# Layer 0: weighing in parts, the image's group norm as its own task, TensorE's chunk work in text order

## The chip, the cores and the metric

The kernel runs on one core of a Trainium2 chip. The metric is the device time of one execution in microseconds, from the runs shown below. All data is 32-bit floating point. The core's engines are TensorE (PE, with its weight load PEld), VectorE (DVE), ScalarE (ACT), GpSimd (POOL) and SyncE (SP), which here issues all data transfers. Each engine works through its own instruction list strictly in order and waits on semaphores for the others.

## The reference

The model has four layers on 16 images of 192 channels and 32 by 32 pixels, each `x = x + layer(group_norm(x))`. The change touches layer 0 alone. Cut to what matters, layer 0 computes for each image (1024 tokens, 12 heads of 32):

```python
x = group_norm(x)                          # 32 groups of 6 channels
h = layernorm(seq)                         # over the 192 channels of a token
x_in, z = split(h @ w_up + b_up)           # 384 each
x_act = silu(causal_conv4(x_in))
q, k, v = x_act @ w_q, x_act @ w_k, x_in
i_pre, f_pre = [q, k, v] @ w_i + b_i, [q, k, v] @ w_f + b_f
# per head and token t:
m   = max(log_sigmoid(f) + m_old, i)
C   = exp(log_sigmoid(f) + m_old - m) * C_old + exp(i - m) * v k^T
n   = the same with k alone
hs  = (C q) / max(|n q|, 1)
hs  = normalise each head of hs;  h_out = (hs + skip * x_act) * silu(z)
x1  = seq + h_out @ w_down + b_down;       x2 = silu(seq @ w_lin + b_lin)
y   = conv3x3(x1 + x2);  batch norm over all images;  leaky relu
```

The other three layers are a selective scan, a depthwise convolution with batch norm, and a four-way selective scan with a local branch.

## The kernel before

**Tiling.** The recurrence of layer 0 is computed in chunks of 128 tokens: 8 an image, 128 in all. Within a chunk the recurrence is a masked, weighted product like attention; between chunks a state of 32 by 33 per head is carried (the 33rd column carries the denominator). Four chunks make a *unit* of 512 tokens (`U`), two units an image. What comes ahead of the recurrence is computed by unit (`layer0_front`): layer norm, `w_up`, the causal convolution `xact` on VectorE (12 passes), `w_lin`, the SiLUs (with two loads of the activation table), `w_q`, `w_k` and the gates (`layer0_gates`). The first unit of an image first loads the image into the tile `x`, of which there is one buffer, and normalises it by groups in place: statistics on VectorE, two small TensorE products (`gnmv`, `gnq`), a power on GpSimd, two passes over `x`.

**One step.** `layer0_step(g)` is one chunk. In the text it has, in order:
- the products `p = s * e` on VectorE, four of them, and `vr = v * e[..., 127]` on GpSimd;
- `layer0_weigh` for chunk g+1: a transfer of the gate row, spread over 128 partitions, into `e` (two buffers); two GpSimd additions (the mask, then `u` of each source token); an Exp on ScalarE;
- with a new unit also `layer0_decays`, eight tiny transposes and three tiny products on TensorE;
- `it = q * state` of the chunk before, then twelve products `num = p * v`, then `h` on VectorE;
- `layer0_state`: `vr * kt` on TensorE, four VectorE instructions for the new `state`;
- `layer0_scores` for chunk g+1: twelve products `s` (k times q), the transposes `kt` and `xin` with their evictions to `kt` (VectorE) and `v` (ScalarE);
- `layer0_output` for chunk g-1: the transposes of `hs`, the products with the gate, `ht`;
- `layer0_norm`: the head norm of `h`: sums on VectorE, `hs` (subtraction) on GpSimd, `sq` on ScalarE, `mhv` on VectorE and ScalarE, `hs` (multiplication) on GpSimd.

When a unit's last chunk is two steps old, `layer0_down` multiplies by `w_down` and writes the image into `ypad`. After an image's two units `layer0_spread` copies `ypad` through memory into `ya` and `yb`, and `layer0_conv2` does the 3 by 3 convolution as 15 taps in three parts.

**What sets the order.** The code does not issue instructions directly: it records them in text order, and a scheduler at compile time writes each engine's list. It goes by text order and by an estimate of when each operand is ready, so that an instruction may be moved ahead of others of its engine. The recorded text order itself comes from two sources. The steps of the chunks are the main line; between their parts (at each `yield`), `Side.tick` advances background tasks. A task is a generator with a kind, a start and an end, counted in steps; it gets its share of parts by the time passed, and `Wait` holds it back. Unit i's front runs from step 4i - 3.9 to 4i - 1.2, an image's convolution over 7.2 steps:

```python
side.add("front", self.layer0_front(i, sp, bp, dp, psum), NCH * i - 3.9, NCH * i - 1.2)
```

**PSUM.** Eight banks: two of `mm`, through which nearly all TensorE results go, four of `s`, one of `num`, one of `conv`. A group that writes `mm` needs the bank of the `mm` group two before it to be read out. `p` has three buffers for four products of a chunk, so that the fourth waits for the first three `num` products.

Of the kernel before, what the change touches and what calls it, by code (L numbers as in the profile page):

```python
# [10 lines left out]
F32 = mybir.dt.float32  # L11
AF = mybir.ActivationFunctionType
# [7 lines left out]
HP = 96  # L20
DI = 384
S = 1024
# [219 lines left out]


class Chunk:

# [15 lines left out]
class Program:  # L261
# [117 lines left out]
    def layer0(self):  # L379
        tc = self.tc  # L380
        with (
# [23 lines left out]
            self.layer0_weigh(chunks[0], bp)  # L405
            finish(self.layer0_scores(chunks[0], bp, psum))
# [80 lines left out]
    def layer0_conv2(self, b, part, bp, psum):  # L487
# [169 lines left out]
    def layer0_decays(self, unit, sp, psum):  # L657

        nc = self.nc
        ps = psum.tile([128, 512], F32, name="mm")  # L660
        u, w = unit["u"].rearrange("p (c t) -> p c t", c=NCH), unit["w"]
        for c in range(NCH):
            for j, t in enumerate((u, w)):
                o = (2 * c + j) * NH
                nc.tensor.transpose(ps[:, o : o + NH], t[:, c], self.k("ident", NH)[:, :NH])
        n = 2 * NCH * NH
        for t in range(3):
            nc.tensor.matmul(
                ps[:, n + t * NCH : n + (t + 1) * NCH], self.k0("sel", NH)[:, t * 128 : (t + 1) * 128], w[:, :, 127],
                start=True, stop=True,  # L670
            )
        uw = unit["uw"] = sp.tile([128, NCH, 2, NH], F32, name="uw")
        nc.vector.tensor_copy(uw, ps[:, :n].rearrange("p (c j h) -> p c j h", c=NCH, j=2))
        dec = unit["dec"] = sp.tile([128, 3, NCH], F32, name="dec")
        nc.vector.tensor_copy(dec, ps[:, n : n + 3 * NCH].rearrange("p (g c) -> p g c", g=3))

    def layer0_weigh(self, k, bp):

        nc = self.nc
        e = k.e = bp.tile([128, NH, 128], F32, name="e")  # L680
        nc.sync.dma_start(e, k.unit["row"][:, k.tok].partition_broadcast(128))
        nc.gpsimd.tensor_tensor(e, e, self.k0("mask")[:, None, :].to_broadcast([128, NH, 128]), ADD)  # L682
        nc.gpsimd.tensor_tensor(e, e, k.unit["uw"][:, k.c, 0][:, :, None].to_broadcast([128, NH, 128]), ADD)  # L683
        nc.scalar.activation(e, e, AF.Exp)  # L684

    def layer0_scores(self, k, bp, psum):
# [5 lines left out]
        for i in range(3):  # L692
            for j in range(4):
                part = slice(32 * j, 32 * j + 32)
                nc.tensor.matmul(k.s[j][:, i], k_[part, i, k.tok], q[part, i, k.tok], start=True, stop=True)
        yield
        k.kt = bp.tile([128, DI], F32, name="kt")
        ps = psum.tile([128, 512], F32, name="mm")
        for t in range(3):
            nc.tensor.transpose(ps[:, t * 128 : (t + 1) * 128], k_[:, t, k.tok], self.k("ident"))  # L700
        nc.vector.tensor_copy(k.kt, ps[:, :DI])
# [3 lines left out]
        for t in range(3):  # L705
            nc.tensor.transpose(
                ps[:, t * 128 : (t + 1) * 128], xin[:, t, 3 + k.tok.start : 3 + k.tok.stop], self.k("ident")
            )
        nc.scalar.copy(k.v[:, :, :DH], ps[:, :DI].rearrange("p (h d) -> p h d", h=NH))
        yield  # L710

    def layer0_step(self, g, n, chunks, sp, bp, psum):
# [8 lines left out]
        if k:  # L721
# [7 lines left out]
            if g + 1 < n:  # L729
                i, c = divmod(g + 1, NCH)  # L730
                new = chunks[g + 1] = Chunk(self.unit[i], c, g + 1)
                if c == 0:
                    self.layer0_decays(new.unit, sp, psum)
                self.layer0_weigh(new, bp)
            yield
            it = None
            if g % (S // 128):
                it = psum.tile([128, 512], F32, name="mm")
                for i in range(3):
                    nc.tensor.matmul(  # L740
                        it[:, i * 132 : (i + 1) * 132], k.unit["q"][:, i, k.tok], chunks[g - 1].state[:, i],
                        start=True, stop=True,
                    )
                h = bp.tile([128, NH, DH + 1], F32, name="h")
# [5 lines left out]
            for j in range(4):  # L750
                for i in range(3):
                    nc.tensor.matmul(num[:, 4 * i + j], p[j][:, i], k.v[:, 4 * i + j], start=True, stop=True)  # L752
# [17 lines left out]
    def layer0_state(self, k, vr, last, bp, psum):  # L770
# [3 lines left out]
        for i in range(3):  # L774
            nc.tensor.matmul(
                ps[:, i * 132 : (i + 1) * 132], k.kt[:, i * 128 : (i + 1) * 128],
                vr[:, 4 * i : 4 * i + 4].rearrange("p j d -> p (j d)"), start=True, stop=True,
            )
        new = k.state = bp.tile([128, 3, 132], F32, name="state")
# [32 lines left out]
    def layer0_output(self, k, bp, psum):  # L812
# [6 lines left out]
        for t in range(3):  # L819
            nc.tensor.transpose(  # L820
                ps[:, t * 128 : (t + 1) * 128], k.hs[:, 4 * t : 4 * t + 4].rearrange("p h d -> p (h d)"), self.k("ident")
            )
        nc.vector.tensor_tensor(
# [4 lines left out]
    def layer0_down(self, unit, psum):  # L828
# [5 lines left out]
        for m in range(2):  # L834
            ps = psum.tile([128, 512], F32, name="mm")
            for k in range(3):
                nc.tensor.matmul(
                    ps[:HP], self.w_down[:, k, m * HP : (m + 1) * HP], unit["ht"][:, k], start=k == 0, stop=k == 2
                )
            nc.vector.scalar_tensor_tensor(  # L840
# [839 lines left out]
```

## Time and profile before

| | |
|---|---|
| median of 3 runs | 17599.51 us (17563.52 to 17607.73) |
| the profiled execution: time | 17603.62 us |
| the profiled execution: span, first to last instruction | 17601.8 us |
| mean granted TensorE clock over the span | 0.943 |
| first and last start of a `num` product | 111.0 and 3981.7 us |
| first instruction of layer 1's scan (L955) | 4159.6 us |

The profile is of one execution. A page gives the busy time of each engine, its share in 40 slices, the costliest groups of instructions and who ended the idle time before them. Windows give the same for any stretch, with the clock that TensorE was granted. The waits name the waiting instruction, the one that released it, the total, how often, and the longest. The timeline gives instructions in order: start, duration, engine, line, tiles out<-in, count, and in brackets the idle time before and its releaser. `L726` is line 726 of the kernel. A TensorE product on 32-bit data shows as two passes, so twelve `num` products are 24 matmuls. Layer 0 fills about the first 4000 us; layers 1 to 3 follow in the rest.

### The profile page before, as it was taken

What the parts mean: (1) busy time and instruction counts of PE and PEld (TensorE: products, weight loads), DVE (VectorE), ACT (ScalarE), POOL (GpSimd) and SP (SyncE); (2) the same over time, 40 slices, a digit from 0 to 9 for tenths busy, and PEclk for the clock granted to TensorE, in tenths of its full rate; (3) what the DMA queues carried; (4) which work ended last, traced back from release to release, by engine and by line L of the source; (5) the groups of instructions that cost most, each with busy time, mean ns of one, the idle gap of its engine ahead of it and who ended that gap; (6) DMA issues with size and microseconds to landing.
All of it is one profiled execution on the core that took longest, in us unless ns stands there. A gap on an engine that the chain in (4) does not pass through costs nothing. (4 is left out here: it accounts for less than half of the span.)

```text
span 17601.8 us, 263080 instructions
## 1 busy us (share of the span) xinstructions
PE 15936.2 (91%) x99452; PEld 11143.2 (63%) x99452; DVE 13342.1 (76%) x14859; ACT 11884.1 (68%) x19637; POOL 11481.6 (65%) x5555
## 2 busy tenths in 40 slices
PE   8988898897988899878999999999999999999998
PEld 4444444444555555546777777777777777777777
DVE  4445554555777777757888888888988888888888
ACT  2222222224666666647888888888888888888888
POOL 3333333333555555546888888788888888888888
PEclk7888888888999999989999999999999999999999
DMA  1111111113333333333233233323323332333232
GB/s 48 40 41 40 44 41 36 41 44 92 119 118 118 115 114 112 109 105 101 94 105 105 86 99 107 98 91 99 107 90 97 101 108 83 99 107 100 90 98 67
DMA packets 890141, 1544.65 MB, mean 88 GB/s; under 512 B 83472, under 2 KB 314653, under 8 KB 879530
## 3 DMA queue, kind: packets, MB, share of 16 engines
q1 hardware_dynamic: 888874, 1527.81, 28.7%
q8 instruction: 788, 12.91, 0.3%
q14 instruction: 479, 3.92, 0.1%
HBM read 1284.22 MB, written 243.27 MB: 87 GB/s over the span
## 5 line engine op out<-in xcount | busy, mean ns | idle before, releaser
L986 POOL TENSOR_TENSOR h<-h,cb 128x1536 f32<-128x1536 f32 x2560 | 8875.8, 3471 | 1423.7 <-DVE h L979 894.0
L955 ACT ACTIVATE da<-dt,neg_a 128x512 f32<-128x512 f32 x7680 | 5266.4, 714 | 1725.5 <-DVE h L979 1658.1
L979 DVE TENSOR_TENSOR_SCAN h<-da,carry,xb 128x512 f32<-128x512 f32 x3840 | 4651.8, 1262 | 648.6 <-PE xb L966 589.4
L997 PE MATMUL y<-const,h 128*128 128x128 f32 x30720 | 4714.3, 276 | 129.4 <-DVE ysum L1437 54.4
L979 DVE TENSOR_TENSOR_SCAN h<-da,xb 128x512 f32<-128x512 f32 x3840 | 4440.2, 1202 | 387.9 <-PE xb L966 270.4
L963 PE MATMUL xb<-const,xbt 128*128 128x128 f32 x23040 | 4072.7, 282 | 417.6 <-DVE h L979 262.7
L935 ACT ACTIVATE xbt<-ut,bt 128x384 f32<-128x384 f32 x7680 | 4174.0, 603 | 242.1 <-PE xb L963 240.4
L963 PEld LDWEIGHTS xb<-const,xbt 128*128 128x128 f32 x23040 | 2755.9, 143 | 1812.2 <-issue 641.9
L997 PEld LDWEIGHTS y<-const,h 128*128 128x128 f32 x30720 | 3682.1, 143 | 322.5 <-issue 264.9
L966 PE MATMUL xb<-diag,ut 128*128 128x128 f32 x15360 | 3015.1, 278 | 0.0
L966 PEld LDWEIGHTS xb<-diag,ut 128*128 128x128 f32 x15360 | 2382.4, 195 | 63.2 <-issue 63.2
L985 POOL COPY carry<-h 128x3 f32<-128x3 f32 x1280 | 251.0, 196 | 1213.9 <-DVE h L979 952.7
L945 POOL TENSOR_TENSOR diag<-const,bt 128x512 f32<-128x512 f32 x640 | 681.8, 1065 | 544.1 <-PE xb L966 348.1
L799 POOL TENSOR_TENSOR hs<-h,mhm 128x384 f32<-128x384 f32 x128 | 108.2, 845 | 1068.3 <-DVE den L804 558.6
L682 POOL TENSOR_TENSOR e<-e,const 128x1536 f32<-128x1536 f32 x128 | 452.4, 3534 | 333.5 <-DMA e<-row 309.2
L684 ACT ACTIVATE e<-e 128x1536 f32<-128x1536 f32 x128 | 189.5, 1481 | 631.4 <-POOL e L683 631.4
L500 PE MATMUL conv<-ya,w_conv 128*64 128x512 f32 (+1 forms) x1152 | 578.6, 706 | 27.8 <-ACT y L506 21.3
L885 PE MATMUL mm<-dbl,w_dt 45*128 45x512 f32 x960 | 534.7, 641 | 33.6 <-DVE v L1459 16.2
L752 PEld LDWEIGHTS num<-v,p 128*128 128x128 f32 x3072 | 448.1, 226 | 78.4 <-issue 61.0
L371 PE MATMUL mm<-lnsq,const 96*96 96x512 f32 (+1 forms) x576 | 352.2, 697 | 143.5 <-ACT lnsq L370 118.1
L548 PE MATMUL mm<-xn,w_up 96*128 96x512 f32 x768 | 427.6, 693 | 45.3 <-DVE ypad L840 32.9
L1140 PE MATMUL mm<-rep,t_dw 96*32 96x512 f32 x2304 | 435.0, 616 | 26.3 <-DMA rep<-xr 20.0
(272 smaller groups left out, 18002.3 us busy)
## 6 DMA issues: line engine op xcount, KB each, us to landing
cb<-row SPq DMA_DIRECT2D x2560, 256.0 KB
rep<-xr SPq DMA_DIRECT2D x384, 331.0 KB
e<-row SPq DMA_DIRECT2D x128, 768.0 KB
rep<-xin SPq DMA_DIRECT2D x384, 256.0 KB
rep<-xr SPq DMA_DIRECT2D x384, 228.8 KB
x<-x SPq DMA_DIRECT2D x48, 768.0 KB
xr<-xin SPq DMA_DIRECT2D x48, 612.5 KB
xr<-xpad SPq DMA_DIRECT2D x32, 867.0 KB
```

The source lines that it names most:

```text
L500: nc.tensor.matmul(o, self.w_c2[:k, t, c0 : c0 + o.shape[0]], src[:k, r0 : r0 + 16, dx : dx + W], start=t == 0, stop=t == 14, skip_group_c ...
L682: nc.gpsimd.tensor_tensor(e, e, self.k0("mask")[:, None, :].to_broadcast([128, NH, 128]), ADD)
L752: nc.tensor.matmul(num[:, 4 * i + j], p[j][:, i], k.v[:, 4 * i + j], start=True, stop=True)
L885: nc.tensor.matmul(ps, w_dt[:, t * 128 : (t + 1) * 128], dbl, start=True, stop=True)
L935: nc.scalar.activation(t[:, c], u.ut[:, c], AF.Copy, scale=u.bt[:, c, n : n + 1])
L945: nc.gpsimd.tensor_tensor(d, ident[:, None, :].to_broadcast([128, 4, 128]), u.bt[:, 3, n : n + 4][:, :, None].to_broadcast([128, 4, 128]), ...
L955: nc.scalar.activation(da[i, t], u.dt[:, t], AF.Exp, scale=u.neg_a(t, n))
L963: in_order(nc.tensor.transpose(xb[i, t][:, c * 128 : (c + 1) * 128], xbt[i][:, c, t * 128 : (t + 1) * 128], ident))
L966: in_order(nc.tensor.matmul(xb[i, t][:, 384:], u.ut[:, 3, t * 128 : (t + 1) * 128], u.diag[n // 4][:, n % 4], start=True, stop=True, skip_ ...
L979: nc.vector.tensor_tensor_scan(hv, dv, xv, 0.0 if first else u.carry_in[:, n, t : t + 1], MUL, ADD)
L986: nc.gpsimd.tensor_tensor(h[i], h[i], u.c.pop(n)[:, None, :].to_broadcast([128, 3, 512]), MUL)
L997: in_order(nc.tensor.matmul(u.y[:, j], h[i][:, t, c * 128 : (c + 1) * 128], ident, is_transpose=True, start=n == 0 and j % 4 == 0, stop=n ...
```

## The change

It has three parts.

1. `layer0_weigh` is taken apart. The transfer of the row (`layer0_row`) stays where the whole was. The two GpSimd additions (`layer0_weigh`) are recorded after the chunk's `num` and `h`, the Exp (`layer0_decay`) after `layer0_state`.
2. An image's load and group norm leave `layer0_front` and become a task `layer0_image` with its own window, from step 8b - 5.1 to 8b - 4, ahead of the front of the image's first unit. Group norm and layer norm now yield inside, so that the main line and other tasks can be recorded between their parts, where they were recorded in one piece before.
3. A class `Chain` ties each TensorE instruction of the main line to the one before it by an ordering edge without a semaphore. The scheduler then cannot exchange them among each other; side work can still be placed between them. The chain holds the decays, `s`, `kt`, `xin`, `it`, `num`, `vr * kt`, the `hs` transposes and `w_down`.

```diff
+class Chain:
+    def __init__(self, tc):
+        self.tc, self.last = tc, None
+
+    def __call__(self, ins):
+        if self.last is not None:
+            why = mybir.DependencyInfo(mybir.DependencyClass.NoSync, mybir.DependencyReason.DATA)
+            self.tc.add_manual_dep(ins.ins, self.last, why)
+        self.last = ins.ins.name
+        return ins
...
+            self.main = Chain(tc)
+            for b in range(1, self.nb):
+                side.add("image", self.layer0_image(b, sp, bp, psum), 8 * b - 5.1, 8 * b - 4)
...
+            finish(self.layer0_image(0, sp, bp, psum))
             finish(self.layer0_front(0, sp, bp, dp, psum))
             self.layer0_decays(self.unit[0], sp, psum)
             chunks = {0: Chunk(self.unit[0], 0, 0)}
-            self.layer0_weigh(chunks[0], bp)
+            self.layer0_row(chunks[0], bp)
+            self.layer0_weigh(chunks[0])
+            self.layer0_decay(chunks[0])
...
+    def layer0_image(self, b, sp, bp, psum):
+        nc = self.nc
+        x = self.image[b] = bp.tile([HP, 2, S], F32, name="x", bufs=1)
+        nc.sync.dma_start(x, self.ins["x"][b].rearrange("(m p) t -> p m t", p=HP))
+        yield Wait(0.2)
+        mean, r, _ = yield from self.group_norm(sp, psum, x)
+        for m in range(2):
+            nc.vector.tensor_scalar(x[:, m], x[:, m], mean[:, m : m + 1], r[:, m : m + 1], SUB, MUL)
...
     def layer0_front(self, i, sp, bp, dp, psum):
-        if first:
-            x = self.image[b] = bp.tile([HP, 2, S], F32, name="x", bufs=1)
-            nc.sync.dma_start(x, self.ins["x"][b].rearrange("(m p) t -> p m t", p=HP))
-            yield
-            mean, r, _ = finish(self.group_norm(sp, psum, x))
-            for m in range(2):
-                nc.vector.tensor_scalar(x[:, m], x[:, m], mean[:, m : m + 1], r[:, m : m + 1], SUB, MUL)
-            yield
         x = self.image[b]
...
-        finish(self.layer_norm(
+        yield from self.layer_norm(
             bp, psum, [x[:, m, tok] for m in range(2)], [xn[:, m] for m in range(2)],
             self.k("ones192", HP), HP, U,
-        ))
-        yield
+        )
...
-    def layer0_weigh(self, k, bp):
-        e = k.e = bp.tile([128, NH, 128], F32, name="e")
-        nc.sync.dma_start(e, k.unit["row"][:, k.tok].partition_broadcast(128))
-        nc.gpsimd.tensor_tensor(e, e, self.k0("mask")[:, None, :].to_broadcast([128, NH, 128]), ADD)
-        nc.gpsimd.tensor_tensor(e, e, k.unit["uw"][:, k.c, 0][:, :, None].to_broadcast([128, NH, 128]), ADD)
-        nc.scalar.activation(e, e, AF.Exp)
+    def layer0_row(self, k, bp):
+        k.e = bp.tile([128, NH, 128], F32, name="e")
+        self.nc.sync.dma_start(k.e, k.unit["row"][:, k.tok].partition_broadcast(128))
+
+    def layer0_weigh(self, k):
+        nc = self.nc
+        nc.gpsimd.tensor_tensor(k.e, k.e, self.k0("mask")[:, None, :].to_broadcast([128, NH, 128]), ADD)
+        nc.gpsimd.tensor_tensor(
+            k.e, k.e, k.unit["uw"][:, k.c, 0][:, :, None].to_broadcast([128, NH, 128]), ADD
+        )
+
+    def layer0_decay(self, k):
+        self.nc.scalar.activation(k.e, k.e, AF.Exp)
...
     def layer0_step(self, g, n, chunks, sp, bp, psum):
...
-                self.layer0_weigh(new, bp)
+                self.layer0_row(new, bp)
             yield
...
                 for i in range(3):
-                    nc.tensor.matmul(num[:, 4 * i + j], p[j][:, i], k.v[:, 4 * i + j], start=True, stop=True)
+                    self.main(nc.tensor.matmul(num[:, 4 * i + j], p[j][:, i], k.v[:, 4 * i + j], start=True, stop=True))
...
+            if new:
+                self.layer0_weigh(new)
             yield
             self.layer0_state(k, vr, chunks.get(g - 1) if g % (S // 128) else None, bp, psum)
+            if new:
+                self.layer0_decay(new)
             yield
```

All other TensorE instructions of the chain are wrapped in `self.main(...)` as `num` is here.

More of the change, by code (lines that the diff above doesn't have):

```diff
@@ L664, in layer0_decays @@
                 o = (2 * c + j) * NH
-                nc.tensor.transpose(ps[:, o : o + NH], t[:, c], self.k("ident", NH)[:, :NH])
+                self.main(nc.tensor.transpose(ps[:, o : o + NH], t[:, c], self.k("ident", NH)[:, :NH]))
         n = 2 * NCH * NH
         for t in range(3):
-            nc.tensor.matmul(
+            self.main(nc.tensor.matmul(
                 ps[:, n + t * NCH : n + (t + 1) * NCH], self.k0("sel", NH)[:, t * 128 : (t + 1) * 128], w[:, :, 127],
                 start=True, stop=True,
-            )
+            ))
         uw = unit["uw"] = sp.tile([128, NCH, 2, NH], F32, name="uw")
@@ L694, in layer0_scores @@
                 part = slice(32 * j, 32 * j + 32)
-                nc.tensor.matmul(k.s[j][:, i], k_[part, i, k.tok], q[part, i, k.tok], start=True, stop=True)
+                self.main(nc.tensor.matmul(k.s[j][:, i], k_[part, i, k.tok], q[part, i, k.tok], start=True, stop=True))
         yield
@@ L699, in layer0_scores @@
         for t in range(3):
-            nc.tensor.transpose(ps[:, t * 128 : (t + 1) * 128], k_[:, t, k.tok], self.k("ident"))
+            self.main(nc.tensor.transpose(ps[:, t * 128 : (t + 1) * 128], k_[:, t, k.tok], self.k("ident")))
         nc.vector.tensor_copy(k.kt, ps[:, :DI])
@@ L705, in layer0_scores @@
         for t in range(3):
-            nc.tensor.transpose(
+            self.main(nc.tensor.transpose(
                 ps[:, t * 128 : (t + 1) * 128], xin[:, t, 3 + k.tok.start : 3 + k.tok.stop], self.k("ident")
-            )
+            ))
         nc.scalar.copy(k.v[:, :, :DH], ps[:, :DI].rearrange("p (h d) -> p h d", h=NH))
@@ L739, in layer0_step @@
                 for i in range(3):
-                    nc.tensor.matmul(
+                    self.main(nc.tensor.matmul(
                         it[:, i * 132 : (i + 1) * 132], k.unit["q"][:, i, k.tok], chunks[g - 1].state[:, i],
                         start=True, stop=True,
-                    )
+                    ))
                 h = bp.tile([128, NH, DH + 1], F32, name="h")
@@ L774, in layer0_state @@
         for i in range(3):
-            nc.tensor.matmul(
+            self.main(nc.tensor.matmul(
                 ps[:, i * 132 : (i + 1) * 132], k.kt[:, i * 128 : (i + 1) * 128],
                 vr[:, 4 * i : 4 * i + 4].rearrange("p j d -> p (j d)"), start=True, stop=True,
-            )
+            ))
         new = k.state = bp.tile([128, 3, 132], F32, name="state")
@@ L819, in layer0_output @@
         for t in range(3):
-            nc.tensor.transpose(
+            self.main(nc.tensor.transpose(
                 ps[:, t * 128 : (t + 1) * 128], k.hs[:, 4 * t : 4 * t + 4].rearrange("p h d -> p (h d)"), self.k("ident")
-            )
+            ))
         nc.vector.tensor_tensor(
@@ L836, in layer0_down @@
             for k in range(3):
-                nc.tensor.matmul(
+                self.main(nc.tensor.matmul(
                     ps[:HP], self.w_down[:, k, m * HP : (m + 1) * HP], unit["ht"][:, k], start=k == 0, stop=k == 2
-                )
+                ))
             nc.vector.scalar_tensor_tensor(
```

## The prediction

> **What bounds the kernel now.** I read the page first, for the stages; then the windows over the middle of layer 0; then TensorE's waits there, as a list and in order of time; then the other engines beside the longest waits. The chain that ended last is of no use: it follows layers 1 to 3.
>
> ```profile
> PE 15936.2 (91%) x99452; PEld 11143.2 (63%) x99452; DVE 13342.1 (76%) x14859; ACT 11884.1 (68%) x19637; POOL 11481.6 (65%) x5555
> PEclk7888888888999999989999999999999999999999
> ...
> 2000.00:2500.00 500.00, 446.25 (x1784) 228.61 (x1784) 254.81 (x446) 139.15 (x206) 181.96 (x110) 0.84 0.17 41
> 2500.00:3000.00 500.00, 448.66 (x1786) 228.62 (x1785) 253.88 (x448) 138.21 (x204) 182.09 (x110) 0.84 0.16 41
> 3000.00:3500.00 500.00, 449.93 (x1796) 230.48 (x1796) 252.18 (x448) 139.37 (x206) 181.75 (x110) 0.85 0.16 41
> ```
>
> The columns of a window are its length, then busy time of PE, PEld, DVE, ACT and POOL, granted clock, DMA share, GB/s. Layer 0 is the first nine to ten slices: the `num` matmuls, one group a chunk, start between 111.0 and 3981.7 us, so 127 steps take 3870.7 us: 30.5 us a step, 243.8 us an image of eight. PE is busy 90%, DVE 51%, POOL 36%, ACT 28%, DMA 16%. So layer 0 is bound by TensorE, but by two losses on it rather than by its work. It idles 1500 - 1344.8 = 155 us in these 1500, and its granted clock is 0.84, while the layers behind hold 0.97. Who ends the idle time:
>
> ```profile
> PE mm L820 <- DVE kt L701: 49.2, 12, 5.7
> PE mm L371 <- ACT lnsq L370: 36.6, 6, 6.4
> PE mm L548 <- DVE ypad L840: 13.4, 6, 3.8
> PE mm L568 <- DVE ypad L840: 12.8, 6, 4.2
> ```
>
> (total us, times, longest us.) All thirteen waits listed sum to 154.6 us: every idle microsecond is named. None is for a chunk's own data; the first, third and fourth are PSUM: `mm` has two buffers, so each group waits until the group two before it has been evicted. What makes an eviction late is seen beside the longest such wait:
>
> ```profile
> 2136.38 0.56 DVE L780 TENSOR_TENSOR state<-mm,const 128x396 f32<-128x396 f32 x1
> 2136.86 2.15 DVE L807 SCALAR_TENSOR_TENSOR mhv<-mhv,den 128x12 f32<-128x12 f32 x1
> 2138.93 5.32 DVE L786 SCALAR_TENSOR_TENSOR state<-state,dec 128x132 f32<-128x132 f32 x3
> 2138.96 3.43 POOL L682 TENSOR_TENSOR e<-e,const 128x1536 f32<-128x1536 f32 x1
> 2144.18 1.47 DVE L726 TENSOR_TENSOR p<-s,e 128x384 f32<-128x384 f32 x3
> 2145.57 0.54 DVE L701 COPY kt<-mm 128x384 f32<-128x384 f32 x1
> 2146.17 0.90 PE L820 MATMUL mm<-const,hs 128*128 128x128 f32 x3 [5.71 <-DVE kt L701]
> ```
>
> DVE's queue reaches the `kt` copy late: gate scans, a state update that a POOL pass stretches, then `p`. The clock's share shows in equal groups of `num` a dozen us apart, and in a window of 13 us that is all at half clock after a wait of only 1.1 us:
>
> ```profile
> 2153.18 2.09 PE L752 MATMUL num<-v,p 128*128 128x33 f32 x18
> 2162.46 0.55 PE L820 MATMUL mm<-const,hs 128*128 128x128 f32 x3 [1.11 <-ACT v L709]
> 2165.64 3.89 PE L752 MATMUL num<-v,p 128*128 128x33 f32 x18
> ...
> 2164.00:2177.00 13.00, 12.45 (x47) 9.85 (x47) 3.66 (x12) 2.06 (x2) 7.14 (x6) 0.50 0.28 67
> ```
>
> A mean of 0.843 between full and half speed is 31% of the time at half clock, 471 us of 1500, of which 90% is busy, 424 us. By the pair above (3.89 / 2.09 = 1.86) that work takes 228 us warm: 196 us of excess. So idle 155 and cold 196 are what could be won in 1500 us. Times 3870.7 / 1500 = 2.58: 400 and 506 us. Layer 0 can gain 906 us at the very most.
>
> **The change, part by part.** *Amount of work.* The built lists of both kernels hold the same instructions on each engine and on the SP queue, and from layer 1 on the same order. Nothing is added or removed; an ordering edge on one engine costs no instruction. All is a matter of order, inside some 3900 us.
>
> *The weighing.* Its two POOL passes (mean 3534 and 2828 ns) and its Exp (1481 ns) are split over the step in the text, but in the built POOL list the passes for chunk g+2 followed `hs` of chunk g before and still do, save that the second `hs` product now often slips between them. The `e` DMA still waits for `p` and `vr` of the chunk two before; once an image it is now queued on SP behind the `yrows` store, which waits for `ypad` (88.0 us in 1500); behind it stands only what also comes after `ypad`. The weighing ends some 15 us before `p` needs it, so I cost this at nothing; were the cover gone, an `e` pass more on the path is 3.5 us a step. On ACT the Exp waited 254.0 us in 1500 for POOL with others queued behind it: between the two `lnsq` squares it held up the second. After, both squares stand together ahead of it. That gain is in the next item.
>
> *The group norm.* Its two small matmuls now stand about a step before the layer norm, and between the mean and the first `lnsq` matmul lie `it`, `num` and `vr` (some 6 us) where there were nine `s` matmuls. The normalisation (two passes of about 1.05 us), the subtraction and the square fit in that. Of 36.6 us I take 31 away; what is late next is `xn` for the first `w_up`, about 1 us. The `x` load keeps its place in SP's list; it still waits for `xl` on POOL (28.9 us).
>
> *TensorE in text order.* Before, the scheduler had pulled parts of `s` and `num` of the next chunk forward, and `w_k`, `w_up` past `vr`. Now a step is always `it`, `num`, `vr`, `s`, `kt`, `xin`, `hs`, with the side work between. I take the four kinds of step in turn, from the end of `num` to the group that needs `kt`'s buffer:
> - Gates step: before, about 8 us of PE work there against 14 us on DVE (5.7 us of wait, above). Now all nine `w_k` (three times 2.8 us) lie behind `num`: 14 us. But `k`'s third eviction now stands behind `p` on DVE, so `xin` waits about 2 us: 5.7 falls to 2; the other half's 0.9 rises to 2.
> - Decays step: 5 to 6 us of PE work before and after, the same DVE list: 1.1 and 3.4 us stay.
> - Layer norm step: about 1 us left; `ypad`'s two DVE passes now come after all of `xact`, but in the built list `w_down` stands after `num` no longer pulled forward, so the POOL pass of the chunk after next no longer starts under `xact` (L560 takes 0.75 us free; one pair of 4.64 us stands beside L682 and L683).
> - `w_lin` step: unchanged, 1 to 1.5 us.
>
> So `kt` saves 13 of 49, `ypad` with `sz` and `xl` half of 38, 19, the rest 5 of 20. With 31: 68 us in 1500. Times 2.58: 175 us.
>
> *The clock.* Fewer waits, fewer half-clock stretches. The decays' tiny matmuls and what stays keep theirs. I take 38% of the excess, somewhat less than the idle's share (68 of 155, 44%): 74 in 1500, times 2.58: 191 us.
>
> **Two rules weighed.** The row says a wait of 1.1 us was followed by 13 us at half clock. The Trainium skill, "TensorE: Matmul & The Clock Gate", Part 1, says the array falls back to half rate after an idle window of about 3.4 us. By the rule only waits of that size count; of those the change surely removes one an image (`lnsq`), with some 10 us at half clock behind it, 4.5 us of excess: 16 times that is 72, and the sum 175 + 72 = 247. By the row it is 366. I take the row. Against the change speaks "SBUF — State Buffer", Who interferes with whom: a DVE instruction with two SBUF inputs and a GpSimd one that reads SBUF exclude each other for the whole instruction. L786 agrees: 0.35 us each free (median), 3.61 at most. Weighing passes placed later in the text could fall on the state update in every step: by that rule up to 3.4 us times 8 an image, 16 images, 435 us lost. By the built POOL list they stand where they stood, so 0.
>
> Sum against the profiled run's own 17603.6 us (its span is 17601.8; the median of the three runs shown, 17599.5, lies 4.1 below): 17603.6 - 175 - 191 = 17237.6, say 17240.
>
> **The rivals.**
> - *Only the group norm pays.* The `lnsq` wait goes (31 times 2.58 = 80) with its cold stretch (72); the rest is traded one wait for another. For it: the `kt` copy stands behind the same DVE work as before. 17603.6 - 152 = 17450.
> - *Nearly all waits go.* If DVE is in time everywhere, three quarters of the 906 us go: 16920. Against: the decays steps, whose lists did not change.
> - *Slower: the fixed order exposes the `kt` eviction.* With `s` no longer pulled ahead, TensorE reaches `xin` and `hs` with nothing to do in between until DVE has done `mhv`, `p` and `kt`; one POOL pass on the state update adds 3.4 us. In half of the 128 steps that is 218 us, and with half of a cold window each (1.7 us) 109 more; less 152 for the group norm: +175, 17780. It decides from 152 / 128 = 1.2 us more of wait and cold per step. For it: DVE 51% busy and strictly in order, the longest wait is already this one. Against: PE work between `num` and `hs` grows or stays in every kind of step.
> - *It does nothing.* The waits move about and sum to the same: 17600.
>
> **How the numbers follow.** My case 0.62, only the group norm 0.14, nearly all 0.07, nothing 0.05, slower 0.12. A difference under 0.3% (53 us) is about what a measurement of this kernel can tell from none. The first three are faster but for 0.01 of the first: 0.82; slower takes the 0.12 and 0.01: 0.13; same 0.05. My case's own range, with between a fifth and two thirds of the 906 us won, is 17000 to 17430. The range for 8 in 10 leaves out the slower case and half of "nearly all": 16960 to 17540.
>
> **What would show it.** In the profile after: PE busy above 92% and a clock near 0.90 in windows of the middle of layer 0; a step of about 27.6 us; no wait of the layer norm's second reduction (L371) on `lnsq` over 1 us; the `kt` wait below 36 us in 1500; layers 1 to 3 within a few us of now. Wrong it is if the clock stays at 0.84 while idle falls, if a wait of `xin` or `hs` appears in every step, or if DVE's L786 has grown.

## The result: 1.2% faster, and the profile after

The changed kernel takes 17375.6 us (median of 4 runs, 17347.8 to 17403.5); the kernel before took 17587.4 in the runs beside it (median of 4, 17563.5 to 17607.7). The ratio is 0.988, 95% interval 0.9858 to 0.9902: 212 us less, where 366 were forecast. The profiled execution took 17403.5 us, its span is 17401.7.

First two rows of the changed kernel's page, busy time by engine and the granted clock in 40 slices:

```profile
PE 15749.6 (91%) x99452; PEld 11013.2 (63%) x99452; DVE 13122.0 (75%) x14859; ACT 11873.6 (68%) x19637; POOL 11450.8 (66%) x5555
PEclk8889998989999999989999999999999999999999
```

And its windows in the middle of layer 0, with the columns of the windows of before:

```profile
2000.00:2500.00 500.00, 447.58 (x1924) 224.74 (x1922) 239.68 (x482) 150.77 (x222) 189.52 (x116) 0.90 0.18 44
2500.00:3000.00 500.00, 444.14 (x1917) 224.47 (x1916) 241.57 (x488) 148.24 (x223) 201.67 (x125) 0.88 0.18 44
3000.00:3500.00 500.00, 446.79 (x1918) 223.94 (x1917) 244.34 (x484) 146.07 (x220) 188.09 (x116) 0.90 0.17 42
```

TensorE's busy time is 447.58 + 444.14 + 446.79 = 1338.5 of 1500 us. It idles 161.5 us, against 155 before: in these windows the idle share did not fall at all. What rose is the granted clock, from 0.84 to 0.89, and with it the number of matmuls done in a window (1917 against 1786). The `num` groups now run from 110.4 to 3754.3 us, 28.7 us a step against 30.5. The first `da` of the layer 1 scan comes at 3932.0 us instead of 4159.6, 227.6 us earlier; from there to the end it takes 13469.7 us, 27 more than before.

TensorE's waits in the changed kernel in the same 1500 us (total us, times, longest us):

```profile
PE mm L377 <- DVE x L543: 48.7, 7, 7.5
PE mm L851 <- ACT v L736: 29.1, 9, 4.3
PE conv L520 <- DMA ya<-yrows: 26.8, 7, 4.6
PE mm L851 <- DVE kt L728: 17.8, 13, 3.4
PE mm L365 <- ACT v L736: 9.1, 7, 1.6
PE mm L733 <- DVE k L613: 8.0, 7, 1.1
```

The wait for `lnsq` (36.6) is gone and the `kt` wait fell from 49.2 to 17.8. In their place stand three that were small or absent: the mean matmul of the layer norm (L377) waits 7 us an image for the normalised `x`, the `hs` transposes (L851) wait for the copy of `v`, the convolution waits for the padded rows `ya`. Who makes `x` late is seen in the changed kernel's timeline around one such wait:

```profile
2059.67 0.15 DVE L367 TENSOR_SCALAR gnr<-mm 96x2 f32<-96x2 f32 x1
2059.83 3.42 POOL L705 TENSOR_TENSOR e<-e,const 128x1536 f32<-128x1536 f32 x1 [2.45 <-DMA e<-row]
2063.33 2.75 POOL L706 TENSOR_TENSOR e<-e,uw 128x1536 f32<-128x1536 f32 x1
2066.03 0.69 POOL L309 TENSOR_TENSOR gnr<-gnr,const 96x2 f32<-96x2 f32 x1
2066.70 0.83 POOL L841 TENSOR_TENSOR hs<-hs,mhv 128x384 f32<-128x384 f32 x1
2066.76 3.80 DVE L543 TENSOR_SCALAR x<-x,gnmean,gnr 96x1024 f32<-96x1024 f32 x2 [5.54 <-POOL gnr L309]
2067.49 0.86 POOL L755 TENSOR_TENSOR vr<-v,e 128x396 f32<-128x396 f32 x1
2068.31 0.99 POOL L857 TENSOR_TENSOR ht<-ht,xact 128x384 f32<-128x384 f32 x1
2069.90 3.73 PE L377 MATMUL mm<-x,const 96*96 96x512 f32 x4 [7.27 <-DVE x L543]
```

The group norm's sum is ready at 2059.8. Its inverse square root (called the root below), 0.69 us on POOL, stands behind the two weighing passes of the chunk after next, 6.2 us. Then the normalisation takes 3.80 us for its two passes, not 2.1: the first takes 3.08 us, while `hs`, `vr` and `ht` run on POOL, and the second 0.80. The mean matmul starts as the first ends. And the same kernel's timeline around a wait of the `hs` transposes:

```profile
2089.22 2.75 POOL L706 TENSOR_TENSOR e<-e,uw 128x1536 f32<-128x1536 f32 x1
2092.00 1.48 ACT L711 ACTIVATE e<-e 128x1536 f32<-128x1536 f32 x1 [7.12 <-POOL e L706]
2093.39 0.46 ACT L736 COPY v<-mm 128x384 f32<-128x384 f32 x1
2093.90 0.90 PE L851 MATMUL mm<-const,hs 128*128 128x128 f32 x3 [3.94 <-ACT v L736]
```

The Exp heads ACT's queue and waits 7.12 us for POOL. The copy of `v`, whose PSUM buffer the `hs` transposes need, stands behind it. Both waits begin at the weighing passes on POOL. The third, for `ya`, was not followed further.

For each kernel below I give an account of the stretch from the first to the last `num` group: its length, TensorE's busy time, its idle time, and how much of the busy time falls into stretches whose granted clock is near half (under 0.9), counted from the trace's clock records and matmul records. A half-clock stretch that is already under way at the first group is left out (9 to 32 us of busy time).

| kernel | length | busy | idle | busy at half clock |
|---|---|---|---|---|
| before | 3871 | 3465 | 406 | 1012 |
| after | 3644 | 3267 | 377 | 684 |

So of the 227 us, 198 are busy time and 29 are idle time, and the busy time is that of the same matmuls (14041 and 14045 in the two stretches). With the 1.86 of the pair of `num` groups, 328 us less at half clock are worth 328 x (1 - 1/1.86) = 152 us of the 198; the other 46 this rough count does not place.

### The profile page after: what moved, and what is told of

It reads as the page before. It is cut to its first block, busy times and chain, and to the rows that moved or that the text cites. A ratio compares the mean times of both kernels' runs of the same rounds, so it can differ in the third digit from the quotient of the medians.

```text
span 17401.7 us, 263068 instructions
## 1 busy us (share of the span) xinstructions
PE 15749.6 (91%) x99452; PEld 11013.2 (63%) x99452; DVE 13122.0 (75%) x14859; ACT 11873.6 (68%) x19637; POOL 11450.8 (66%) x5555
## 5 line engine op out<-in xcount | busy, mean ns | idle before, releaser
L854 DVE TENSOR_TENSOR ht<-sz,mm 128x384 f32<-128x384 f32 x128 | 70.7, 552 | 519.5 <-PE mm L851 519.5
L779 PEld LDWEIGHTS num<-v,p 128*128 128x128 f32 x3072 | 389.3, 201 | 102.2 <-issue 77.9
L920 DVE SCALAR_TENSOR_TENSOR dt<-lnsq,mm 128x512 f32<-128x512 f32 x480 | 322.0, 671 | 171.9 <-ACT lnsq L919 171.9
```

## The experiments

Three groups of runs, each beside its own runs of the kernel before (medians 17573.2, 17567.9 and 17613.4 us). Between groups the ratios to before are compared, not the microseconds.

### Text order, or the image as a task?

*chain_only*: the kernel after with the image task undone; it keeps the text order of TensorE's chunk instructions and the split weighing.

```
-  side.add("image", self.layer0_image(b, ...), 8 * b - 5.1, 8 * b - 4)
-  finish(self.layer0_image(0, sp, bp, psum))
   (load, group norm, normalisation and layer norm at the head of
    layer0_front again, each in one piece, as before the change)
```

> The kernel before with TensorE's chunk instructions chained alone; weighing and group norm as before. Theory (contiguous chunk groups are the gain: s and num in one piece, fewer half-clock stretches): the lnsq wait of some 6 us an image stays, but s falls from 224 us of TensorE time to about 150, and the time is 120 to 200 us under the kernel before, near 17430. Rival (the group norm's own task is the gain): within 50 us of the kernel before.

*image_only*: the image task and the layer norm in pieces, without the text order, the weighing in one piece.

```
   def __call__(self, ins):
-      if self.last is not None:
+      if False:
...
+      self.layer0_weigh(new)   # right behind layer0_row(new), and
+      self.layer0_decay(new)   # no longer behind num and state
```

> The group norm's task and the yields inside the norms alone; no chain, weighing as before. In its built TensorE list most of s and num stand in one piece too, with one or two chunks an image still cut. Theory (contiguity): nearly as fast as with all three parts, 17380 to 17450, with the wait on x in place of the one on lnsq. Rival (the chain is the gain): within 50 us of the kernel before, about 17590.

| kernel | us | ratio to before (95%) | length | busy | idle | busy at half clock |
|---|---|---|---|---|---|---|
| chain_only | 17505.7 | 0.9961 (0.9949 to 0.9974) | 3774 | 3382 | 391 | 913 |
| image_only | 17357.8 | 0.9878 (0.9863 to 0.9892) | 3629 | 3335 | 294 | 867 |

The image task alone gives the whole ratio of the change (0.988). The text order alone gives 67 us, and on top of the image task nothing: there it takes 68 us from the busy time (of which 684 us are at half clock instead of 867) and adds 83 us of idle time, so that the lengths come out alike. Part of that idle time is the `hs` transposes' wait for `v`, 5.3 us in image_only's chunk loop and 65.3 us in the changed kernel's. Four of chain_only's waits in 2000 to 3500 us:

```profile
PE mm L855 <- DVE kt L734: 47.7, 12, 5.7
PE mm L739 <- ACT q L617: 26.9, 6, 5.3
PE mm L377 <- DVE x L554: 24.1, 12, 3.6
PE mm L385 <- ACT lnsq L384: 4.0, 2, 2.1
```

And three of image_only's:

```profile
PE mm L733 <- DVE xn L389: 30.1, 7, 4.8
PE mm L377 <- DVE x L543: 21.7, 7, 5.4
PE mm L849 <- DVE kt L728: 18.9, 13, 2.6
```

In chain_only the `kt` wait is 47.7 us in 1500, as before: the text order did not shorten it. It did take the `lnsq` wait to 4.0 us, which was expected to stay; waits for `q` and `x` came up in its place. The weighing split has no part in it either: with the image task in and the text order out, the built lists with and without the split are the same on every engine.

### Which half of the image task?

*one_piece*: image_only with the layer norm of every unit issued in one piece again.

```
-  yield from self.layer_norm(...)
+  finish(self.layer_norm(...))
+  yield
```

> The image's load, group norm and normalisation stay a task of their own, in pieces, six steps or so ahead of their use; the layer norm of every unit is again issued in one piece, as before the change. TensorE's chunk instructions are not put in text order and the weighing is not split (as in the run image_only, 17358 us). If the gain of the image task comes from the lead that the normalised image now has over its first reader, this kernel keeps it: 17340 to 17400 us, and no wait for the squares worth naming at the first unit of an image. If the gain comes from the layer norm's mean and variance being issued at different times, this kernel loses it: the variance matmul waits for the squares again (some 30 us in 1500) and the time is 17480 us or more. Mixed: both halves give part, 17400 to 17480.

*norm_pieces*: image_only with the load, group norm and normalisation back at the head of the front, and only the layer norm in pieces.

> The other half alone: the image's load, group norm and normalisation are back at the head of the front, the group norm in one piece; only the layer norm is issued in its two pieces, mean and differences first, squares and variance one slot later. No text order, weighing not split. If the layer norm in pieces carries the gain: 17340 to 17420 us, with the wait of the variance matmul for the squares gone. If the image's lead carries it: 17520 to 17590 us, near before. If the two are additive parts, the savings of this kernel and of one_piece against before (17573) should add to about 215 us.

| kernel | us | ratio to before (95%) | length | busy | idle | busy at half clock |
|---|---|---|---|---|---|---|
| one_piece | 17351.8 | 0.9877 (0.9858 to 0.9895) | 3612 | 3362 | 250 | 904 |
| norm_pieces | 17460.5 | 0.9937 (0.9922 to 0.9953) | 3702 | 3370 | 332 | 891 |

The lead of the image carries the gain: 0.9877 without any piece-wise layer norm. The pieces alone give half as much, and nothing on top of the lead. Each half frees the variance matmul of the `lnsq` wait: in one_piece it is 1.9 us in 1500, in norm_pieces it is not listed. The two halves cure the same wait, which fits that they don't add up (216 and 107 us). Their busy times are nearly the same; what the lead has over the pieces is less idle time, part of it at `kt` (13.4 us in 1500 against 36.3).

### The wait for the normalised image

*root_act*: the kernel after with the root of the group norm on ScalarE, which takes it out of POOL's queue.

```
-  self.pow_mhalf(r)
+  nc.scalar.activation(r, r, AF.Ln)
+  nc.scalar.activation(r, r, AF.Exp, scale=-0.5)
```

> The changed kernel with the group norm's inverse root of layer 0 taken by two ScalarE instructions (Ln, Exp) in place of the GpSimd power, which stood 6 us behind the weighing passes of a chunk. Theory (the wait of the mean matmul on x, 7.3 us an image, is this queue, and its half-clock stretch goes with it): that wait falls to 1 to 4 us, 70 to 150 us less than the changed kernel, 17230 to 17310. Rival (the normalisation on DVE is then held by the weighing pass itself[...]): the wait falls by less than 3 us and the time by less than 50 us.

*filler*: the kernel after with seven more matmuls an image ahead of the mean matmul, whose results nobody reads. They fill the wait for `x` and keep TensorE busy, but nothing else comes earlier.

```
   (behind the normalisation of every image but the first)
+  ps = psum.tile([128, 512], F32, name="mm")
+  for _ in range(7):
+      self.main(nc.tensor.matmul(ps[:HP], ones192, w_up[:, 0, :512], ...))
```

> The changed kernel with seven unread matmuls of 96 by 512 put ahead of each image's mean matmul, where TensorE waits 7.3 us for x: 14 passes of 0.43 us, 6 us of useless work inside the wait; no data is needed sooner or later. Theory (a wait costs its own length and then a stretch at half clock): idle falls by 6 us an image, the half-clock stretch of some 17 us that starts there goes, and the time falls by 40 to 100 us against the changed kernel, to about 17300. Rival (only idle time counts, the clock is lost to the thin chunk matmuls): the time stays within 30 us of 17376 or rises by up to 40.

*image_root*: image_only with the root on ScalarE.

> The image task and the pieces without the text order, and the group norm's root taken on ScalarE (as in the run root_act) instead of on GpSimd. Root_act, which has the text order as well, took 17286 us. If the text order adds nothing once the image is a task of its own: this kernel is within 25 us of root_act, 17265 to 17310. If the text order is worth something like the 67 us it gave alone, and in the changed kernel lost it to the queue on GpSimd in front of the root: this kernel is slower than root_act by 40 us or more, 17325 to 17360, little below image_only's 17358, whose wait for the normalised image was only 21.7 us in 1500.

| kernel | us | ratio to before (95%) | length | busy | idle | busy at half clock |
|---|---|---|---|---|---|---|
| root_act | 17285.6 | 0.9834 (0.9821 to 0.9847) | 3561 | 3248 | 313 | 649 |
| filler | 17366.4 | 0.988 (0.9866 to 0.9894) | 3617 | 3325 | 292 | 617 |
| image_root | 17300.0 | 0.9845 (0.9828 to 0.9863) | 3593 | 3314 | 279 | 817 |

Taking the root out of POOL's queue is worth 0.46% by the ratios, about 80 us. The wait it shortens, in root_act's list of TensorE's waits in 2000 to 3500 us:

```profile
PE mm L381 <- DVE x L547: 31.3, 7, 4.9
PE mm L855 <- ACT v L740: 27.2, 7, 4.3
PE conv L524 <- DMA ya<-yrows: 21.0, 6, 4.0
```

From 48.7 to 31.3: the normalisation itself is left, 1868 ns a pass on average over layer 0. Its passes now run beside other POOL work: 12 of the 32 take 2.49 us beside the second weighing pass and `hs`, 12 take 1.31 us beside `hs` and `vr`. Filler removes the wait for `x` altogether, idle falls by 85 us, the mean clock of its profiled run rises from 0.951 to 0.955, and the time stays: the ratio is 0.988 for both, with overlapping intervals. Its account says why. With the seven matmuls the busy time rises by 58 us net, and the busy time at half clock falls by only 67 us, of which about 0.46 (1 - 1/1.86, from the pair of `num` groups) is gained. A higher mean clock over work that nobody needs is not a gain.

Image_root lies within root_act's interval: with the root off POOL, too, the text order adds nothing.

### The copy of v ahead of the Exp

The remaining waits of root_act name `v` and `ya`. *best* takes both on: root_act, the convolution's pieces 0.4 step later, and an edge that puts the Exp of a chunk behind the copy of the same chunk's `v` on ACT.

```
-  at = 8 * b + 9.6 + 2.4 * j
-  side.add("conv", self.layer0_conv2(b, j, bp, psum), at, at + 2.4)
+  at = 8 * b + 10 + 2.3 * j
+  side.add("conv", self.layer0_conv2(b, j, bp, psum), at, at + 2.3)
...
-  nc.scalar.copy(k.v[:, :, :DH], ...)
+  k.vcopy = nc.scalar.copy(k.v[:, :, :DH], ...)
...
   def layer0_decay(self, k):
+      ins = self.nc.scalar.activation(k.e, k.e, AF.Exp)
+      if hasattr(k, "vcopy"):
+          self.tc.add_manual_dep(ins.ins, k.vcopy.ins.name, NoSync)
...
   (layer0_decay(new) behind layer0_scores(new) in layer0_step)
```

> Root_act (17286 us) with two more waits of the changed kernel taken away: the convolution's three pieces begin 0.4 step later, so that its padded rows have landed (the first of them waited 26.8 us in 1500), and the copy of v is put ahead of the Exp of the same chunk on ScalarE (the transposes of hs waited 29.1 us in 1500 for it). If idle time of TensorE in this layer is paid for one to one and both waits go without a successor: up to 144 us less, 17140 to 17190. If each wait hands half of its time to the next one, as the change's own did: 17200 to 17250. If the layer is bound by something else by now: 17270 to 17300.

The parts of it were then run one by one, and the edge on the kernel before as well. *v_first* is the kernel after with the edge alone; *conv_late* is root_act with the later convolution alone; *v_nochain* is image_root with the edge; *v_before* is the kernel before with the edge alone (the Exp as a function of its own, behind the scores).

> The changed kernel with one order altered: on ScalarE the copy of v stands ahead of the Exp of the same chunk. TensorE's order is the changed kernel's but for a few places. Best, which has this, the later convolution and the root on ScalarE, took 16984 us, 301 below root_act, though its convolution still waits 32 us in 1500 for its padded rows. If the place of the v copy carries the 301: 17060 to 17120 us (changed kernel 17376 less 260 to 310), the hs wait (110.8 us of the chunk loop) down to some 15 us, half-clock stretches from 843 us to under 400 us. If the later convolution carries half of it: 17200 to 17260.

> Root_act (17286 us) with only the convolution begun 0.4 step later. Since the wait for the padded rows did not go in the run best, which has this too: 17265 to 17305 us, no difference, and half-clock stretches near root_act's 751 us. If the later convolution is what raised the clock in best: 17130 or less.

> The image task, the pieces and the root on ScalarE without the text order (image_root, 17300 us), with the copy of v ahead of the Exp. If the text order adds nothing here either: 16980 to 17050 us, like best. If the text order is what made the hs transposes wait for v in the changed kernel (110.8 us, against 39.2 us without it), the copy of v has little to free here: 17250 to 17300, and the text order with v ahead is then worth some 250 us that the changed kernel never showed.

> The kernel before with the copy of v ahead of the Exp on ScalarE and nothing else. Its hs transposes waited 149.5 us in the chunk loop. If they wait for the same copy: 17300 to 17400 us, more than the change brought. If they waited for other things (kt on VectorE, which is late there under the weighing passes): 17480 to 17570, little or nothing.

| kernel | us | ratio to before (95%) | length | busy | idle | busy at half clock |
|---|---|---|---|---|---|---|
| best | 16984.0 | 0.9665 (0.9649 to 0.9681) | 3250 | 3044 | 205 | 250 |
| v_first | 17253.8 | 0.9796 (0.9781 to 0.981) | 3545 | 3252 | 293 | 682 |
| conv_late | 17256.7 | 0.9799 (0.9785 to 0.9814) | 3493 | 3174 | 319 | 500 |
| v_nochain | 17169.9 | 0.9751 (0.9735 to 0.9767) | 3427 | 3234 | 193 | 652 |
| v_before | 17174.9 | 0.975 (0.9731 to 0.9769) | 3461 | 3252 | 210 | 588 |

Best beats both kernels: 3.3% below before, 2.2% below the change by the ratios. Its gain over root_act, about 300 us, is twice the upper end of what its two waits were expected to pay. Two of its windows:

```profile
2000.00:2500.00 500.00, 469.15 (x2164) 242.94 (x2157) 259.00 (x546) 170.47 (x259) 222.62 (x134) 0.96 0.19 50
2500.00:3000.00 500.00, 476.42 (x2203) 241.54 (x2201) 254.13 (x539) 167.75 (x252) 214.00 (x130) 0.97 0.19 47
```

And the longest of its waits between 2000 and 3500 us (its chunk loop ends at 3360; the second line is of layer 1):

```profile
PE conv L524 <- DMA ya<-yrows: 32.2, 8, 6.7
PE mm L1191 <- issue: 19.0, 1, 19.0
PE mm L812 <- POOL xin L565: 17.1, 6, 4.7
```

The clock in the middle of layer 0 is 0.96 to 0.97, as in the layers behind it. Of root_act's two longest waits neither `x` nor `v` is left among the longest; `ya` still is, though the convolution begins later. So that part of the expectation failed as a mechanism: the later convolution did not take its wait away. It does pay by itself (conv_late 0.9799 against root_act's 0.9834, no difference was expected): in the chunk loop its `ya` wait is 51.0 us (root_act 52.5), its `hs` wait fell from 100.1 to 63.3 and its busy time at half clock from 649 to 500. Most of the fall at `hs` is in the share that waits for `kt` (37.2 to 10.5 us). Why `hs` waits less for it when the convolution is later was not settled.

ACT's rows for the Exp tell what the edge does (busy us, mean ns, then idle time before them and who ended it, in the same 1500 us). In the kernel before:

```profile
L684 ACT ACTIVATE e<-e 128x1536 f32<-128x1536 f32 x48 | 71.1, 1481 | 254.0 <-POOL e L683 254.0
```

In the changed kernel:

```profile
L711 ACT ACTIVATE e<-e 128x1536 f32<-128x1536 f32 x52 | 77.1, 1482 | 159.9 <-POOL e L706 159.7
```

In v_before:

```profile
L687 ACT ACTIVATE e<-e 128x1536 f32<-128x1536 f32 x54 | 80.3, 1488 | 0.0
```

With the edge the Exp never waits at the head of ACT's queue: POOL is done when its turn comes. In v_first, where TensorE's list is the changed kernel's but for a few places, the `hs` wait of the chunk loop falls from 110.8 to 17.1 us. But `x` is late there as in the changed kernel (47.6 us in 1500, up to 7.6), and the busy time at half clock stays (682 against 684); v_first gains 0.8% where 1.5 to 1.8% was expected. In best, with both waits gone, the half-clock time collapses to 250. That they are gone is not enough for it: v_nochain has neither any more, idles no longer than best (193 against 205), and still has 652.

V_before was expected to be worth nothing, or 17300 to 17400 us, 1.2 to 1.8% below its own runs of before; it is worth 2.5%, twice what the change brought, with the edge alone. Its TensorE waits, 2000 to 3500 us:

```profile
PE mm L827 <- DVE kt L707: 30.9, 10, 3.9
PE mm L587 <- ACT xact L576: 11.8, 13, 1.0
PE mm L363 <- DVE x L528: 9.0, 7, 2.7
PE mm L371 <- ACT lnsq L370: 4.3, 2, 2.2
```

The `lnsq` wait, which the change was there to pay by, fell from 36.6 to 4.3, and the wait for `x` is 9.0 where the changed kernel has 48.7. In the same group of runs v_first, which is v_before plus the whole change, is 79 us slower than v_before, and the intervals of the two ratios don't overlap. So the change's 1.2% and the edge's 2.5% are not two gains: both free the layer norm, and the change brings the root's place in POOL's queue with it. V_nochain, which has the image task and the edge with the root on ScalarE, equals v_before, and fell between its two expectations. Best lies 0.86% below v_nochain, all of it in busy time (3044 against 3234 us): its half-clock stretches are nearly as many (43 against 51) and half as long (6.8 us against 13.5 on average). Of the 0.86% the later convolution was worth 0.35% on root_act. Whether the rest is the text order, now that `x` and `v` are in time, no run separates. That is left open, as is how the edge frees `lnsq` in v_before: its TensorE and DVE lists differ from before's in several hundred rows, since the scheduler answers to the edge.

## Why the prediction was right, and which steps were wrong

The direction was right, the range held, and the size was off by 154 us: 212 measured, 366 forecast (the profiled runs: 200).

- *The clock term met its number, and partly by luck.* 191 us were forecast; the busy time of the chunk loop fell by 198, and the middle windows show 0.90, 0.88, 0.90 where "near .90" was written. But the term was drawn from the idle time: "Fewer waits, fewer half-clock stretches", 38% of the excess because 44% of the idle time was to go. Idle time fell by 7% (29 of 406 us), which by the same working is about 30 us (an estimate: 0.07 x 0.38 / 0.44 x 506). What changed is the size of the waits. Those of 1.2 to 3.4 us fell from 73 (148 us) to 37 (68 us) in the chunk loop, those over 3.4 us rose from 37 (194 us) to 46 (227 us), and the half-clock stretches fell from 116 to 79. Of the two rules weighed there, the row was nearer: 72 us for the clock by the rule of the Trainium skill ("TensorE: Matmul & The Clock Gate", Part 1, an idle window of about 3.4 us), 191 by the row. In the trace of before, of 36 waits of 1.2 to 2.0 us that began at full clock, 28 were followed within 6 us by a half-clock stretch, so waits well below 3.4 us count here. That the rule's sum, 247, lies nearer to 212 than the row's 366 is an accident of the other term.
- *The idle term was wrong.* 175 us were forecast, 29 measured. The step that failed is the group norm's: "The normalisation (two passes of about 1.05 us), the subtraction and the square fit in that. Of 36.6 us I take 31 away; what is late next is `xn` for the first `w_up`, about 1 us." The `lnsq` wait did go. What was late next was `x`, by 48.7 us. The task was followed on TensorE and on SP's queue, not on POOL's: there its root of 0.69 us was moved behind 6.2 us of weighing. And the 1.05 us a pass was a mean of unlike passes: in the trace of before the first of a pair takes 1.31 us beside `hs` on POOL in 13 of 16 images, the second 0.80. In the changed kernel 13 of the 16 first passes take 3.07 to 3.08 us beside `hs`, `vr` and `ht`. Root_act shows the first part: about 80 us back.
- *The Exp was read and not followed to its end.* The prediction had the 254.0 us that ACT waits at the Exp "with others queued behind it" and looked only at the second square. There it never waited: in the trace of before the Exp stands between the squares in 14 of 32 units, with no idle time ahead of it. The copy of `v` is in the same queue, and `hs` needs its buffer: 9.1 us before, 29.1 after.
- *The four kinds of step in text order explain nothing.* They priced how a fixed TensorE order shortens the `kt` wait. It is 17.8 us, below the 36 forecast, but image_only without the text order has 18.9, and chain_only with it 47.7. The number was met for another reason: the image task.
- *The weighing split at nothing* was right. *L786 grown* was feared and did not come: the state update's mean fell from 836 to 451 ns, `xact`'s from 1109 to 748 ns (as forecast). What POOL falls on instead in the changed kernel is the normalisation, 1180 to 1960 ns a pass, through `hs`, `vr` and `ht` rather than the weighing passes.
- *The rival "only the group norm pays", 17450,* had the right part of the change, at 152 us where image_only gained 215. *The slower case* did not come: the `kt` wait shrank.
- *Layers 1 to 3 within a few us* was 27 us off. Over the 14 kernels here, whose later layers are the same code, that part took from 13432 to 13470 us in the profiled runs; the kernel before has 13442, the changed one the top value, and conv_late, with the change in it as well, 13466. V_first and root_act, which have it too, lie at 13440 and 13437, so it is scatter rather than a cost of the change.

## What to carry to other kernels

Follow a moved task through every queue that it uses, and price it there by what stands ahead of it, however short it is: a root of 0.69 us behind two long passes cost about 80 us. An instruction that heads an in-order queue and waits for a slow engine holds up all behind it, and the wait turns up under other names: look for the row with the longest idle time of an engine "that is not the bottleneck", and ask who stands behind it. Before adding up two gains, ask whether they cure the same wait; here four edits each took the `lnsq` wait below 5 us in 1500 (text order, pieces, lead, the edge), and they paid 0.4, 0.6, 1.2 and 2.5%. So the wait that an edit removes does not tell by itself what it pays.

## What was not expected of the hardware

Half-clock stretches do not follow from single waits alone. Waits of 2.0 to 3.4 us that began at full clock were followed by one in 20 of 23 cases before, 11 of 11 after, 20 of 21 in best; waits of 0.3 to 0.7 us in none of 39 before, but in 19 of 54 after, where other waits lie close by. In all three every record of the granted clock but one in each lasts a whole multiple of 3.413 us. Taking single waits away moved the half-clock time little (684 to 682 in v_first, 649 in root_act). Nor does the count of long waits tell it: v_nochain has 21 waits of 2 us and more and 652 us at half clock, best has 35 and 250.

The normalisation of `x`, a `tensor_scalar` with one large SBUF input, is slowed by POOL as the two-input state update is. DVE's row over layer 0, in the kernel before:

```profile
L527 DVE TENSOR_SCALAR x<-x,gnmean,gnr 96x1024 f32<-96x1024 f32 x32 | 36.5, 1180 | 10.8 <-POOL gnr L295 10.8
```

And in the changed kernel:

```profile
L543 DVE TENSOR_SCALAR x<-x,gnmean,gnr 96x1024 f32<-96x1024 f32 x32 | 61.5, 1960 | 56.3 <-POOL gnr L309 56.3
```

The Trainium skill, "SBUF — State Buffer", Who interferes with whom, names `tensor_scalar` among the operations that can enter a mode with two ports and then contend; the trace of the changed kernel agrees: the 15 passes with no POOL instruction beside them took 0.80 to 0.81 us, the 13 beside `hs`, `vr` and `ht` 3.07 to 3.08.
